# Every fourteenth group's first 128 rows fetched by SyncE, one row at a time

## The chip, the cores and the metric

The kernel runs on one core of a Trainium2 chip. A core has five engines, each with an instruction queue of its own: TensorE (PE in the profile, its weight loads PEld), VectorE (DVE), ScalarE (ACT), GpSimd (POOL) and SyncE (SP). SP computes nothing: here it issues transfers and waits for semaphores. Sixteen DMA engines carry out the transfers that the engines issue. Instructions of one engine go in order, and engines wait for each other by semaphores. The metric is the device time of one execution in microseconds (us), as a median of runs.

## The reference

A graph of 12,500 nodes with 128 features each and 200,000 edges, which are sorted by their destination node. Two layers follow a normalisation, and their result is added to the input:

```python
h = jnp.maximum(_layernorm(x, axis=-1), 0.0)
...
deg = jax.ops.segment_sum(jnp.ones_like(edge_weight_raw), dst, num_segments=N)
wsum = jax.ops.segment_sum(edge_weight_raw, dst, num_segments=N)
w = edge_weight_raw / jnp.maximum(wsum, EPS)[dst]
feat = jax.nn.relu(node_features @ W_pool + b_pool)
msg = feat[src] * w[:, None]
neigh = jax.ops.segment_max(msg, dst, num_segments=N)
neigh = jnp.where(deg[:, None] > 0, neigh, 0.0)
rst = node_features @ W1_self + neigh @ W1_neigh + b1
...
h = jax.nn.relu(rst)
msg2 = h[src] * w[:, None]
neigh2 = jax.ops.segment_sum(msg2, dst, num_segments=N) / jnp.maximum(deg, 1.0)[:, None]
out = jax.nn.relu(h @ W2_self + neigh2 @ W2_neigh + b2)
```

Layer 1 takes for each node the maximum of the weighted rows of its incoming edges' sources (`feat[src]`), layer 2 their weighted sum (`h[src]`). In both, 200,000 rows of 128 numbers (512 bytes) are read from a table in the chip's memory, in an order that only the input `src` tells.

## The kernel before

**Tiling.** The edges are cut into 391 groups of 512 (`NG`, the last with 320), and a group into four chunks of 128 (`Q`), one edge per partition. Nodes are worked on in 98 tiles of 128. The tables of the two layers are `feat_d` and `h_d`, each in the chip's memory.

**Gathers.** `gather` (L499 to L510) has GpSimd fetch the rows of a group into a buffer `gt`: one indirect DMA for each chunk (L507), whose 128 indices are a column of `srcT`. `sources` (L488 to L495) makes `srcT` in the preparation, from the loaded list of sources `sr`, in four parts: VectorE converts a part to floats (L491), TensorE transposes it, ScalarE writes it. SyncE isn't concerned with gathers.

**The ring.** `buffer` (L132) gives a group its place in a ring of buffers: 18 groups deep at first, then 14, then 11 (`full`), as tiles that were lent to it go back to other uses. Layer 2 has 11 throughout. GpSimd issues the gathers of group i as soon as the group that had that buffer has been read by TensorE, and so runs ahead of the other engines by as much as the ring is deep.

**Layer 1** is one loop over i (L860 to L980) whose order is written out by hand, since nothing reorders instructions there. Groups before 17 (`FIRST`) were gathered from x in the preparation; groups 17 to 390 are gathered from `feat_d` (L877). In iteration i TensorE transposes the four chunks of group i into PSUM (L896). VectorE multiplies by the edge weights `gs` (L940) and, one iteration later, takes the running maximum over each destination's edges with a scan (L911), with the marks `kt` that say where a destination begins. Two and more iterations later come transposes back (L952), a copy of ScalarE (L906), a product that picks each destination's last row (L961) and its copy into a window of the aggregate (L849). Finished node tiles pass through `nodes1` (L751 to L782), which stores `h_d` (L778).

**Layer 2** is a loop over i (L1050 to L1080). Group i is gathered from `h_d` (L1052), VectorE makes a small selection matrix with the weights in it (L996, L1001), TensorE multiplies each chunk by it one iteration later (`window_product`, L1008), and VectorE adds the result into the aggregate, at an address from a register (`window_add`, L1013; registers are loaded eight at a time, L729). Finished tiles pass through `nodes2` (L793 to L806), which stores the output four tiles at a time (L806); the input for the last addition is loaded four tiles at a time (L787).

**What SyncE does.** In layer 1 it issues in each iteration the load of `gs` for the next group (L583: 256 KB, three buffers, so it waits until L940 has used the group before the previous), every fourth iteration the load of `kt` (L589, 512 KB), and the stores of `h_d`. In layer 2 it issues L787 and L806 alone. A DMA that SyncE issues takes one of eight completion semaphores in turn; an engine that needs the data of several DMAs waits for each of their semaphores.

Of the kernel before, what the change touches and what calls it, by code (L numbers as in the profile page):

```python
# [7 lines left out]
F32 = mybir.dt.float32  # L8
# [30 lines left out]
LEAST = LESS + 4 * MID  # L39
KEPT = 4  # L40
PAIR = 2
PART = 24
PART_AT = (0, 1, 9, 17)
ADDED = PART_AT[-1] + PART
# [5 lines left out]
def gnn_kernel(ctx, tc, x, src, dst, ew, w_pool, b_pool, w1s, w1n, b1, w2s, w2n, b2, out):  # L50
# [29 lines left out]
    h_d = dram.tile([NP, D], F32, name="h_d")  # L80
    keep_d = dram.tile([NT * P, G], BF16, name="keep_d")
    s_d = dram.tile([2, NP], F32, name="s_d")

    one_way, other_way = (const.tile([P, NP + LW], F32, name=f"way_{i}") for i in range(2))
    h0T, h1T = (a[:, :NP].rearrange("p (t n) -> p t n", n=P) for a in (one_way, other_way))
# [402 lines left out]
    def sources():  # L488
        for t in range(NT):
            f = wk.tile([P, G], F32, name="sf")  # L490
            nc.vector.tensor_copy(f, sr[:, t, :])  # L491
            pt = columns(pq, f, Q)
            yield
            nc.scalar.activation(srcT[:, t], pt, AF.Copy)
            yield  # L495

    def edges_of(g):
# [4 lines left out]
    def gather(gt, table_d, g, only=None, last=None):  # L502

        t, r, ne, chunks = edges_of(g)
        limit = {} if last is None else dict(bounds_check=last, oob_is_err=False)
        for j, k in chunks if only is None else chunks[only:only + 1]:
            nc.gpsimd.indirect_dma_start(  # L507
                out=gt[:k, j, :], out_offset=None, in_=table_d[:, :],
                in_offset=bass.IndirectOffsetOnAxis(ap=srcT[:k, t, j, r:r + 1], axis=0), **limit)
        return gt  # L510
# [174 lines left out]
    def background():  # L685
# [8 lines left out]
            yield NG, fitness, t  # L694
        yield NG, lambda get, t: verdict(get), 0

    def pairs_of(g):
# [115 lines left out]
    with tc.manual_schedule(), tc.tile_pool(name="ew", bufs=3) as wk, \  # L813
# [3 lines left out]
        def side_step():  # L817

            while jobs:
                due, steps = jobs[0]  # L820
                if next(steps, jobs) is jobs:
                    jobs.pop(0)
                elif i < due:
                    break

        pms, scs, sels, prs, rws, pas = ({} for _ in range(6))
        turn = turns(wide1, 6)
        busy = {}

# [36 lines left out]
        for i in range(max(turn) + 6):  # L866
# [7 lines left out]
            if i % KEPT == 0 and i and i + 2 < NG:  # L874
                keep_rows(i + 2, keep_tile())
            if FIRST <= i < NG:
                gts[i] = gather(buffer(i, True), feat_d, i)  # L877

            if i + 1 < NG:
                weight_rows(i + 1, wk.tile([P, G], F32, name="gs"))  # L880
# [2 lines left out]
            if i < FIRST:  # L883
                if i > 0:
                    nc.scalar.activation(pms[i], raws.pop(i).rearrange("p q n -> p (q n)"), AF.Relu, bias=bp_col)
                if i + 1 < FIRST:
                    raw_columns(pn, i + 1)
                if i + 2 < FIRST:
                    raw_scale(i + 2)
                    raw_norm(i + 2)  # L890
                if i + 1 < FIRST:
                    raw_back(i + 1)
            elif i < NG:
                gt = gts.pop(i)
                for j, k in edges_of(i)[3]:
                    nc.tensor.transpose(pms[i][:, j * P:j * P + k], gt[:k, j, :], ident[:k, :k])  # L896
            if NG - 2 <= i < NG:
                window_copy(due(5))

# [73 lines left out]
                raw_stats(i + 3)  # L973
            if i >= FIRST and i % 3:
                side_step()
        assert not busy
        i = NG
        side_step()
# [4 lines left out]
    with tc.manual_schedule(), tc.tile_pool(name="ew2", bufs=3) as wk, \  # L983
            tc.tile_pool(name="ep2", bufs=2, space=PSUM) as ps:
        place = ps.tile([P, 2, Q, PART], F32, bufs=1)
        hit, iota = place[:, 0], place[:, 1]
        flip = ps.tile([P, 2, P], F32, bufs=1)
        for j, at in enumerate(PART_AT):
            nc.vector.tensor_copy(iota[:, j, :], cols[:, 0, at:at + PART])

        nc.vector.memset(agg2, 0.0)
        ss, pas, xrs = ({} for _ in range(3))

        def places(g):
            t, r, _, _ = edges_of(g)
            nc.vector.tensor_tensor(hit, iota, locT[:, t, :, r:r + 1].to_broadcast([P, Q, PART]), OP.is_equal)  # L996

        def weighted(g):
            t, r, _, _ = edges_of(g)
            ss[g] = wk.tile([P, Q, PART], F32, name="s")  # L1000
            nc.vector.tensor_tensor(ss[g], hit, w2T[:, t, :, r:r + 1].to_broadcast([P, Q, PART]), OP.mult)  # L1001

        def window_product(g):
            chunks = edges_of(g)[3]
            pas[g] = ps.tile([P, ADDED], F32, name="pa", bufs=3)
            gt, s = gts.pop(g), ss.pop(g)
            for j, k in reversed(chunks):
                nc.tensor.matmul(pas[g][:, PART_AT[j]:PART_AT[j] + PART], gt[:k, j, :], s[:k, j, :],  # L1008
                                 start=j == len(chunks) - 1, stop=j == 0, skip_group_check=True)

        def window_add(g, at):
            n = ADDED if g < GF else PART_AT[len(edges_of(g)[3]) - 1] + PART
            nc.vector.tensor_tensor(agg2[:, bass.ds(at, n)], pas.pop(g)[:, :n], agg2[:, bass.ds(at, n)], OP.add)  # L1013

        sbs = []
        for e in range(EARLY):
            sbs.append(wk.tile([P, G], I32, name=f"sb{e}", bufs=1))
            nc.sync.dma_start(sbs[e], src[None, e * G:(e + 1) * G].to_broadcast([P, G]))

        def early_groups():  # L1020

            for e in range(EARLY):
                one = dr.bitcast(F32)[:, :LATE, :G]
                for k in range(LATE):
                    nc.vector.tensor_scalar(one[:, k, :], sbs[e], late_nodes[:, k:k + 1], None, op0=OP.is_equal)
# [24 lines left out]
        for i in range(max(turn) + 2):  # L1050
            if EARLY <= i < NG:
                gts[i] = gather(buffer(i, False), h_d, i)  # L1052
                places(i)
            if EARLY <= i < NG:
                weighted(i)
            if i + 4 in turn:
                n = turn[i + 4]
                if n % wide2(n) == 0:
                    xr = x_rows(wk, n, wide2(n), 2)
                xrs[n] = xr  # L1060
            if late is not None:
                stages(late)
                late = None
            if i in turn:
                n = turn[i]
                late = nodes2(wk, ps, n, wide2(n), strided(agg2, n, wide2(n)), xrs.pop(n))
                next(late)
            g = i - 1
            if EARLY <= g < NG:
                window_product(g)  # L1070
            if i >= EARLY and i % 2:
                next(first_groups, None)
            if i == NG - 1:
# [128 lines left out]
```

## Time and profile before

| | us |
|---|---|
| median of 3 runs (4643.74 to 4653.1) | 4652.45 |
| the profiled execution | 4650.7 |
| its span, first to last instruction | 4648.7 |
| layer 1, gathers of L507 from `feat_d` into the ring | 190.3 to 2363.3 |
| layer 2, gathers of L507 from `h_d` into the ring | 2417.3 to 4623.6 |
| granted TensorE clock, mean of the span | 0.527 |

The profile is of one execution. A group row gives line, engine, operation, output and input, how often, busy time in all, mean nanoseconds of one, the idle time of the engine before these instructions and what ended most of it. In a timeline a row begins with the start and the duration in us, and ends with the idle time before it, in brackets. "Issue" is time in which an engine waited for nothing that the profile shows; "remote" is a releaser that the profile can't name. Rows of SPq and similar are instructions of an engine's queue, such as the issue of a DMA: not the transfer itself.

### The profile page before, as it was taken

The page shows a single profiled execution, that of the slowest core. Times are in us where ns is not written, and L with a number is a line of the kernel's source. Part 1 is how long each engine was busy: PE and PEld are TensorE (multiplying, and loading weights), DVE is VectorE, ACT ScalarE, POOL GpSimd, SP SyncE. Part 2 cuts the span into 40 slices and gives each one's busy share as a digit, 9 for nine tenths or more (in the row PEclk, how much of TensorE's full clock was granted, in tenths as well). Part 3 has the DMA queues.
Part 4 walks back from the last instruction along what each step waited for, and adds up shares of the span by engine and source line. Part 5 has one row for each costly group of instructions (what it writes and reads, how often), then busy time and mean ns, then how long its engine had stood idle before and what let it go on. Part 6 is the DMA issues. An engine that isn't in the chain of part 4 may idle for free.

```text
span 4648.7 us, 32678 instructions
## 1 busy us (share of the span) xinstructions
PE 1995.1 (43%) x8700; PEld 1817.3 (39%) x8700; DVE 1741.8 (37%) x5165; ACT 416.0 (9%) x1509; POOL 2953.3 (64%) x3143
## 2 busy tenths in 40 slices
PE   3654543444444444444453344334334333334334
PEld 2444433443434343433342334333334333333334
DVE  3676655765666566665560111111101111111111
ACT  3531111111111111111110000000000000000000
POOL 5356666666666666666646666666666666666665
PEclk8665555555555555555555555555555555555555
DMA  4333443444444444444431112112111111211111
GB/s 130 109 114 116 126 117 103 125 117 114 118 115 120 115 117 116 119 116 117 113 100 46 47 47 62 51 50 56 50 52 53 51 52 51 55 51 52 53 54 45
DMA packets 196303, 397.11 MB, mean 85 GB/s; under 512 B 60703, under 2 KB 69790, under 8 KB 196112
## 3 DMA queue, kind: packets, MB, share of 16 engines
q0 software_dynamic: 100032, 204.97, 17.3%
q1 hardware_dynamic: 95344, 189.06, 13.2%
q8 instruction: 73, 1.20, 0.1%
q10 hardware_dynamic: 736, 0.92, 0.1%
q14 instruction: 118, 0.97, 0.1%
HBM read 374.96 MB, written 19.77 MB: 85 GB/s over the span
## 4 chain that ended last, share of the span: by engine, by line
another core or an unknown queue 23%; issue 23%; PE 20%; POOL 19%; DVE 13%; DMA 1%; ACT 1%; POOLq 0%; ACTq 0%; DVEq 0%
POOL gt L507 18%; PE pa L1008 5%; PE pm L896 5%; DVE pm L911 4%; PE pn L961 4%; DVE pm L940 2%; PE pr L952 2%; DVE sc L936 1%; DVE sc L933 1%; DMA gt<-h_d,srcT 1%; DVE sel L922 1%; PE pn L743 1%; PE pf L643 1%; PE pn L780 1%
## 5 line engine op out<-in xcount | busy, mean ns | idle before, releaser
L507 POOL DMA_INDIRECT gt<-h_d,srcT x1551 | 1463.9, 944 | 743.6 <-issue 419.6
L507 POOL DMA_INDIRECT gt<-feat_d,srcT x1303 | 1230.0, 944 | 680.5 <-issue 294.5
L1008 PE MATMUL pa<-s,gt 128*128 128x24 f32 x3102 | 685.3, 382 | 734.4 <-remote 561.1
L1008 PEld LDWEIGHTS pa<-s,gt 128*128 128x128 f32 x3102 | 682.0, 330 | 748.7 <-remote 567.8
L1013 DVE TENSOR_TENSOR way<-pa,way 128x41 f32 x391 | 78.0, 199 | 1866.9 <-remote 1323.6
L896 PE MATMUL pm<-ident,gt 128*128 128x128 f32 (+1 forms) x1303 | 349.7, 423 | 521.5 <-issue 314.3
L940 DVE TENSOR_TENSOR pm<-pm,gs 128x512 f32<-128x512 f32 x390 | 271.1, 695 | 694.6 <-remote 529.1
L911 DVE TENSOR_TENSOR_SCAN pm<-kt,carry,pm 128x512 f32<-128x512 bf16 x389 | 496.3, 1276 | 4.0
L961 PEld LDWEIGHTS pn<-sel,rows 128*128 128x128 f32 x1564 | 368.8, 324 | 230.8 <-ACT way L849 128.2
L896 PEld LDWEIGHTS pm<-ident,gt 128*128 128x128 f32 (+1 forms) x1303 | 235.8, 218 | 560.4 <-issue 338.5
L961 PE MATMUL pn<-sel,rows 128*128 128x48 f32 x1564 | 358.2, 377 | 217.4 <-ACT way L849 121.9
L743 PE MATMUL pn<-w_2n,way 128*128 128x128 f32 x192 | 74.4, 491 | 601.3 <-issue 325.9
L743 PEld LDWEIGHTS pn<-w_2n,way 128*128 128x128 f32 x192 | 52.8, 323 | 620.2 <-issue 406.6
L906 ACT ACTIVATE rows<-pr 128x256 f32<-128x256 f32 x392 | 149.7, 383 | 1532.8 <-remote 662.1
L952 PE MATMUL pr<-ident,sc 128*128 128x128 f32 x782 | 241.8, 411 | 8.0 <-issue 3.9
L922 DVE TENSOR_SCALAR sel<-cols,lastT,invT 128x48 f32<-128x48 f32 x782 | 243.6, 312 | 0.0
L933 DVE COPY sc<-pm 128x256 f32<-128x256 f32 x391 | 162.6, 416 | 109.5 <-remote 85.9
L952 PEld LDWEIGHTS pr<-ident,sc 128*128 128x128 f32 x782 | 167.2, 224 | 11.5 <-issue 6.1
L936 DVE COPY_PREDICATED sc<-kt,pm 128x256 f32<-128x256 int16 x389 | 168.5, 433 | 4.9 <-issue 4.9
L507 POOL DMA_INDIRECT w2T<-feat_d,srcT x100 | 94.3, 943 | 105.8 <-DVE raw_mv L521 52.0
L780 PE MATMUL pn<-ident,h 128*128 128x128 f32 x94 | 41.9, 446 | 236.8 <-DVE ss L765 73.0
L780 PEld LDWEIGHTS pn<-ident,h 128*128 128x128 f32 x94 | 17.3, 184 | 270.1 <-issue 217.2
(273 smaller groups left out, 2079.6 us busy)
## 6 DMA issues: line engine op xcount, KB each, us to landing
gs<-in_edge_weight SPq DMA_DIRECT2D x389, 256.0 KB
kt<-keep_d SPq DMA_DIRECT2D x97, 512.0 KB
gt<-h_d,srcT POOLq DMA_INDIRECT x1551
gt<-feat_d,srcT POOLq DMA_INDIRECT x1303
feat_d<-fr SPq DMA_DIRECT2D x24, 256.0 KB
xr<-in_x SPq DMA_DIRECT2D x24, 256.0 KB
out<-o SPq DMA_DIRECT2D x24, 256.0 KB
h_d<-h SPq DMA_DIRECT2D x47, 128.0 KB
```

What stands on the lines that cost most here:

```text
L507: nc.gpsimd.indirect_dma_start(out=gt[:k, j, :], out_offset=None, in_=table_d[:, :], in_offset=bass.IndirectOffsetOnAxis(ap=srcT[:k, t, j, ...
L743: nc.tensor.matmul(po, nT, W[neigh_w], start=False, stop=True)
L896: nc.tensor.transpose(pms[i][:, j * P:j * P + k], gt[:k, j, :], ident[:k, :k])
L906: nc.scalar.activation(rws[g][:k, j, :], pr[:k, j, :], AF.Copy)
L911: nc.vector.tensor_tensor_scan(pm[:, :ne], kt[:, :ne], pm[:, :ne], carry, op0=OP.add, op1=OP.max)
L922: nc.vector.tensor_scalar(part, cols[:k, 1, :], lastT[:k, t, j, r:r + 1], invT[:k, t, j, r:r + 1], op0=OP.is_equal, op1=OP.mult)
L933: nc.vector.tensor_copy(sc[:, :ne // 2], two[:, :, 1])
L936: nc.vector.copy_predicated(sc[:, :ne // 2], new[:, :, 1], two[:, :, 0])
L940: nc.vector.tensor_tensor(pms[i][:, :n], rows[:, :n], ws.pop(i)[:, :n], OP.mult)
L952: nc.tensor.transpose(prs[g][:k, j, :], sc[:, j * P:j * P + k], ident)
L961: nc.tensor.matmul(pas[g], rows[:k, j, :], sel[:k, j, :], start=j == 0, stop=j == len(chunks) - 1)
L1008: nc.tensor.matmul(pas[g][:, PART_AT[j]:PART_AT[j] + PART], gt[:k, j, :], s[:k, j, :], start=j == len(chunks) - 1, stop=j == 0, skip_group ...
```

## The change

In preparation, `sources` also multiplies each source index by 512, its row's place in bytes in a table, and stores the four parts to a new table `at_d` in the chip's memory. A new class `Rows` takes chunk 0 of every fourteenth group away from the gathers: groups 37, 51, … 373 in layer 1 (25) and 20, 34, … 384 in layer 2 (27). For each such group g SyncE loads its 128 places, 512 bytes, into a small tile `listed`, at the end of iteration g - 18. In iterations g - 16 to g - 3 it then issues 128 DMAs of one row of 512 bytes each, nine or ten in an iteration, from the place that a register holds into one partition of a tile `single`; sixteen registers are loaded at a time (`BURST`). `single` and `listed` have two places each, used in turn. TensorE reads `single` instead of `gt` for chunk 0 of these groups, in both layers; their other three chunks, and all other groups, are gathered as before.

```diff
@@ sources
             nc.scalar.activation(srcT[:, t], pt, AF.Copy)
+            place = wk.tile([P, G], I32, name="sa")
+            nc.vector.tensor_scalar(place, sr[:, t, :], float(4 * D), None, op0=OP.mult)
+            nc.sync.dma_start(at_d[t * P:(t + 1) * P, :], place)
             yield
@@ gather
         for j, k in chunks if only is None else chunks[only:only + 1]:
+            if any(c.j == j and c.takes(g) for c in besides):
+                continue
             nc.gpsimd.indirect_dma_start(
@@ new
+    class Rows:
+
+        def __init__(self, wk, table, plane, every, first, end):
+            self.single = wk.tile([P, 2, D], F32, name="single", bufs=1)
+            self.listed = wk.tile([1, 2, P], I32, name="listed", bufs=1)
...
+            for c, g in enumerate(range(first, end, every)):
+                self.place[g] = c % 2
+                begin = g - every - 2
+                assert begin >= 2
+                self.plan.setdefault(begin - 2, []).append((self.load, g, 0))
+                for e in range(P):
+                    self.plan.setdefault(begin + e * every // P, []).append((self.fetch, g, e))
...
+        def rows(self, gt, g, j):
+            return self.single[:, self.place[g], :] if j == self.j and self.takes(g) else gt[:, j, :]
+
+        def load(self, g, _):
+            row = self.plane * NT * P + g
+            nc.sync.dma_start(self.listed[:, self.place[g], :], at_d[row:row + 1, self.j * P:(self.j + 1) * P])
+
+        def fetch(self, g, e):
+            if e % BURST == 0:
+                _, self.held = nc.values_load_multi_w_load_instructions(
+                    self.listed[:, self.place[g], e:e + BURST], [mybir.EngineType.SP], min_val=0,
...
+            at = self.held[e % BURST].with_bounds(min_val=0, max_val=(N - 1) * 4 * D, guaranteed_mod_val=0,
+                                                  out_of_modulus=4 * D)
+            nc.sync.dma_start(self.single[e:e + 1, self.place[g], :].bitcast(U8),
+                              self.flat[None, :].bitcast(U8)[:, bass.ds(at, 4 * D)])
+
+        def turn(self, i):
+            for step, g, e in self.plan.get(i, ()):
+                step(g, e)
@@ layer 1
+        byrow = Rows(wk, feat_d, 0, 14, FIRST + 14 + 6, NG - 4)
...
-                gts[i] = gather(buffer(i, True), feat_d, i)
+                gts[i] = gather(buffer(i, True), feat_d, i, besides=(byrow,))
...
-                    nc.tensor.transpose(pms[i][:, j * P:j * P + k], gt[:k, j, :], ident[:k, :k])
+                    nc.tensor.transpose(pms[i][:, j * P:j * P + k], byrow.rows(gt, i, j)[:k], ident[:k, :k])
...
+            byrow.turn(i)
@@ layer 2
+        byrow = Rows(wk, h_d, 0, 14, 14 + 6, NG - 4)
...
-                gts[i] = gather(buffer(i, False), h_d, i)
+                gts[i] = gather(buffer(i, False), h_d, i, besides=(byrow,))
...
-                nc.tensor.matmul(pas[g][:, PART_AT[j]:PART_AT[j] + PART], gt[:k, j, :], s[:k, j, :],
+                nc.tensor.matmul(pas[g][:, PART_AT[j]:PART_AT[j] + PART], byrow.rows(gt, g, j)[:k], s[:k, j, :],
...
+            byrow.turn(i)
```

More of the change, by code (lines that the diff above doesn't have):

```diff
@@ L41 @@
 PAIR = 2
+BURST = 16
 PART = 24
@@ L82, in gnn_kernel @@
     s_d = dram.tile([2, NP], F32, name="s_d")
+    at_d = dram.tile([NT * P, G], I32, name="at_d")
     one_way, other_way = (const.tile([P, NP + LW], F32, name=f"way_{i}") for i in range(2))
@@ L500, in edges_of, with gather @@
         return *divmod(g, P), ne, [(j, min(P, ne - j * P)) for j in range(-(-ne // P))]
-    def gather(gt, table_d, g, only=None, last=None):
+    def gather(gt, table_d, g, only=None, last=None, besides=()):
         t, r, ne, chunks = edges_of(g)
@@ L695, in background, with takes @@
         yield NG, lambda get, t: verdict(get), 0
+    class Rows:
+        def __init__(self, wk, table, plane, every, first, end):
+            self.single = wk.tile([P, 2, D], F32, name="single", bufs=1)
+            self.listed = wk.tile([1, 2, P], I32, name="listed", bufs=1)
+            self.plane, self.flat, self.j, self.place, self.plan, self.held = \
+                plane, table.rearrange("n d -> (n d)"), 0, {}, {}, {}
+            for c, g in enumerate(range(first, end, every)):
[5 more added lines that the diff above has]
+                    self.plan.setdefault(begin + e * every // P, []).append((self.fetch, g, e))
+        def takes(self, g):
+            return g in self.place
+        def rows(self, gt, g, j):
[7 more added lines that the diff above has]
+                    self.listed[:, self.place[g], e:e + BURST], [mybir.EngineType.SP], min_val=0,
+                    max_val=(N - 1) * 4 * D,
+                    skip_runtime_bounds_check_because="sources of edges are nodes, as the gathers have it")
+            at = self.held[e % BURST].with_bounds(min_val=0, max_val=(N - 1) * 4 * D, guaranteed_mod_val=0,
[5 more added lines that the diff above has]
+                step(g, e)
     def pairs_of(g):
```

## The prediction

> **What bounds the kernel now.** I read the busy table and the slices of the page first, then the costliest groups.
>
> ```profile
> PE 1995.1 (43%) x8700; PEld 1817.3 (39%) x8700; DVE 1741.8 (37%) x5165; ACT 416.0 (9%) x1509; POOL 2953.3 (64%) x3143
> ...
> DVE  3676655765666566665560111111101111111111
> ...
> POOL 5356666666666666666646666666666666666665
> ...
> another core or an unknown queue 23%; issue 23%; PE 20%; POOL 19%; DVE 13%; DMA 1%; ACT 1%; POOLq 0%; ACTq 0%; DVEq 0%
> ...
> L507 POOL DMA_INDIRECT gt<-h_d,srcT x1551 | 1463.9, 944 | 743.6 <-issue 419.6
> L507 POOL DMA_INDIRECT gt<-feat_d,srcT x1303 | 1230.0, 944 | 680.5 <-issue 294.5
> ```
>
> POOL is the busiest, at the same six tenths through both layers, and it does little but gather. The chain of waits names no bound: 23% of it ends at releasers that it can't name. So I looked at POOL's own rhythm, in the timeline of POOL in layer 2.
>
> ```profile
> 3436.67 0.94 POOL L507 DMA_INDIRECT gt<-h_d,srcT  x1 [0.30 <-issue]
> 3437.92 0.94 POOL L507 DMA_INDIRECT gt<-h_d,srcT  x1 [0.30 <-issue]
> 3439.17 0.94 POOL L507 DMA_INDIRECT gt<-h_d,srcT  x1 [0.30 <-issue]
> 3444.63 0.94 POOL L507 DMA_INDIRECT gt<-h_d,srcT  x1 [4.52 <-remote]
> ```
>
> A gather occupies POOL for 0.94 us, then 0.30 us pass: 1.25 us from start to start, 5.0 us for the four of a group. Now and then a longer stall comes (4.52 us here), at the first gather of a group: there POOL waits for a buffer of the ring. The windows give the pace with the stalls in it (first row: a special stretch, below; second: layer 1; third: layer 2; columns: PE, PE weight loads, DVE, ACT, POOL, clock, DMA share, GB/s).
>
> ```profile
> 802.00:824.70 22.70, 10.70 (x54) 9.31 (x54) 17.57 (x45) 5.17 (x19) 0.00 (x0) 0.58 0.31 90
> 850.00:2360.00 1510.00, 686.88 (x3012) 614.34 (x3010) 914.25 (x2276) 190.44 (x810) 987.30 (x1047) 0.51 0.42 117
> 2420.00:4624.00 2204.00, 848.55 (x3736) 817.91 (x3736) 272.93 (x1263) 0.00 (x0) 1461.32 (x1549) 0.50 0.19 52
> ```
>
> Layer 1: 1510 / 1047 = 1.442 us per gather, 5.77 us per group. Layer 2: 2204 / 1549 = 1.423, so 5.69. DVE is 61% busy in the one and 12% in the other, yet the pace is the same: what is common to both is POOL. The special stretch decides it. From 801.9 to 824.76 POOL stands still, because the ring shrinks there from 14 groups to 11. The consumers then run alone, on stored groups:
>
> ```profile
> 800.98 0.94 POOL L507 DMA_INDIRECT gt<-feat_d,srcT  x1 [0.30 <-issue]
> 824.76 0.94 POOL L507 DMA_INDIRECT gt<-feat_d,srcT  x1 [22.84 <-PE pm L896]
> ...
> 810.88 1.08 PE L896 MATMUL pm<-ident,w2T 128*128 128x128 f32 x4 [8.04 <-issue]
> 814.40 1.09 PE L896 MATMUL pm<-ident,w2T 128*128 128x128 f32 x4
> ...
> 820.98 1.08 PE L896 MATMUL pm<-ident,w2T 128*128 128x128 f32 x4 [1.84 <-issue]
> 824.04 1.09 PE L896 MATMUL pm<-ident,gt 128*128 128x128 f32 x4 [0.83 <-PE pn L961]
> ```
>
> PE begins a group every 3.1 to 3.5 us there, against 5.77 on the average. So POOL sets the pace and not PE, DVE or the weight loads of SP. The stalls on the ring's buffers do not contradict this: PE gives buffers back in bursts, around POOL's own pauses.
>
> ```profile
> 3429.77 1.87 PE L1008 MATMUL pa<-s,gt 128*128 128x24 f32 x8 [5.91 <-remote]
> 3444.40 0.20 DVE L1013 TENSOR_TENSOR way<-pa,way 128x41 f32 x1 [14.73 <-remote]
> 3445.17 1.02 PE L1008 MATMUL pa<-s,gt 128*128 128x24 f32 x4 [13.53 <-remote]
> ```
>
> After 3431.6 PE has no matmul until 3445.17, while POOL gathers on until 3440.1; then POOL stops, DVE and PE go on at 3444.4 and 3445.2, and POOL resumes at 3444.63. A stall is thus a tax on running far ahead, some 0.7 to 0.8 us a group (5.69 and 5.77 less 5.0).
>
> **The change part by part.** *Removed:* chunk 0 of 25 groups in layer 1 (37, 51, … 373) and 27 in layer 2 (20, 34, … 384), 52 of POOL's 3,143 instructions. Bounds of what one is worth: nothing, if the stall of the ring grows by what POOL saves; 1.25 us, if the stalls stay; 1.42 to 1.44 us, if the stalls shrink in proportion. For all 52: 0, 64.9, or 25 x 1.442 + 27 x 1.423 = 74.5 us. I take 64.9: the nearest row is the uninterrupted pitch, and the stall is as likely to stay as to shrink. What is late next is POOL still, with 55 gathers for 14 groups instead of 56.
>
> *Added on SP:* 128 fetches for each such group, 6,656 in all, over 14 iterations, thus 9.14 an iteration; a register load for every 16; 52 loads of a 512-byte list. These go at the end of iteration i, behind SP's own gs, kt, h_d, xr and out transfers of that iteration, and ahead of the next gs. No such fetch is in the trace. Nearest rows (timeline of SP, one-row transfers of the edge lists; groups of DMAs; register loads of eight values):
>
> ```profile
> 133.46 0.34 SPq L159 DMA_DIRECT2D dr<-in_dst  x1
> 133.84 0.25 SPq L165 DMA_DIRECT2D dr<-in_dst  x1
> 126.50 0.33 SPq L603 DMA_DIRECT2D feat_d<-fr  x1
> 126.87 0.44 SPq L159 DMA_DIRECT2D dr<-in_dst  x1
> ...
> L583 SPq DMA_DIRECT2D gs<-in_edge_weight x390: 327/328/793, 166.6 to 2391.2; - x195
> L589 SPq DMA_DIRECT2D kt<-keep_d x98: 320/327/435, 166.2 to 2387.5; - x98
> L729 DVEq TENSOR_LOAD <-bases x49: 593/596/1056, 2430.3 to 4625.9; - x49
> ```
>
> A one-row transfer is issued in 0.25 us, one of many rows in 0.33, or 0.44 when it follows another at once; 0.04 us lie between two (126.50 + 0.33 to 126.87). One load of eight registers is 0.60 us on DVE; for sixteen I estimate 0.6 to 1.2, so 0.04 to 0.08 a row. Low: 0.25 + 0.04 + 0.04 = 0.33 us a row. High: a row priced like the costliest gs issue, 0.79, and load: 0.87. I take 0.44, between the one-row record and a back-to-back transfer, with 0.04 gap and 0.06 load less the 0.10 by which one row is cheaper. SP's own work for 14 groups of layer 1 is 14 x (0.33 + 0.04) + 3.5 x 0.37 = 6.5 us, with under 1 us of others. With 128 x 0.44 = 56 it makes 63 of the 14 x 5.70 = 80 us that the new pace leaves; the point from which it no longer fits is (80 - 6.5) / 128 = 0.57 us a row. So I cost SP's rows at nothing: POOL's gathers cover them, and where that cover is gone, a row costs what it exceeds 0.57 by.
>
> [...]
>
> Queues that the rows are moved past: SP waits most of its time, and for DVE, one group after another, before each gs.
>
> ```profile
> SPq L583 <- DVE pm L940: 732.5, 121, 14.5
> SPq L806 <- DVE o L802: 548.4, 7, 97.3
> ```
>
> The rows of iteration i are queued behind those waits, so they go out only when DVE has got to group i - 2 of layer 1. The last ones for group g are of iteration g - 3, and PE needs them some four groups after that wait: 12 us or more, against 4 us of issue for nine rows. In layer 2 an out store holds SP for up to 97 us until DVE is there; it comes each 16 groups, and SP then issues 146 rows (64 us by the price taken) while the groups take 91. The gs load of the next group comes 4 us later than before; it has three buffers, 17 us, so nobody waits.
>
> *Added waits:* PE waits for a group's rows on up to eight semaphores, at the transposes and at the products of chunk 0. Behind them are that group's other work on PE, and through the ring POOL. A wait already satisfied is small change:
>
> ```profile
> L896 PEldq EVENT_SEMAPHORE  x374: 51/2946/13117, 283.8 to 2395.1; - x187
> L491 DVE CAST sf<-w2T x4: 417/418/426, 6.9 to 117.0; 128x512 f32<-128x512 int32 x4
> ```
>
> Seven more at 0.05 us are 0.36 us for 52 groups, 19 us at the outside, of which I take 2, since PE has 2 us a group to spare. The preparation gains four multiplies of the size of the cast above (0.42 us each) and four stores (0.33 us of issue): 0 to 5 us, taken as 3, because DVE is not full there (three and six tenths in its first two slices).
>
> Sum: the execution profiled took 4650.7 us (span 4648.7), 1.8 below the median of the runs, 4652.45. 4650.7 - 64.9 + 2 + 3 = **4591 us**.
>
> **Rivals.** *A, the time comes back as ring waits.* POOL reaches the full ring sooner and waits for PE's next burst. For it: the stalls sit at the first gather of a group and end with PE, remote waits of 470 us in all:
>
> ```profile
> POOL gt L507 <- remote: 470.1, 224, 7.5
> ```
>
> Against it: the consumers alone need 3.1 us. If a saved gather gave 40% back, it would be 52 x 0.75 = 39 us, 4617; if all, 4650.7 + 5 = 4656, no change.
>
> *B, SP becomes the bound, slower.* From 0.57 us a row the rows set the pace of PE, and POOL waits for the ring. At 0.62 a group takes (6.5 + 128 x 0.62) / 14 = 6.13 us, 0.40 over the mean of 5.73, for some 377 + 387 groups less the 40 outside the schedule: +290, thus 4940; at 0.60, 5.95 and +160, 4810; at the high end of 0.87 about 6,600. For it: a price with a register as offset isn't shown, and it needs only 0.13 more than I take. Against it: 0.25 for a one-row transfer.
>
> *C, completions in the way.* While POOL gathers, PE's progress stands for 13 us (above). If 9 small completions an iteration hold it in the same manner, each stall grows. Stalls are 0.7 us a group; with 14 completions where there were five, I price it at a third of that more, 0.24 us for 720 groups: +170 less 65, 4755. Against it: the special stretch, in which DMA moved 90 GB/s without POOL, went smoothly, and layer 1, with far more SP transfers, stalls hardly more than layer 2.
>
> That the rows aren't taken off POOL at all I exclude: the gather skips the chunk where it is issued.
>
> **How the numbers follow.** Forecast 0.57 (4572 to 4612: from 4650.7 less the 74.5 of shrinking stalls and 4 of noise, to the start of A); A 0.20, of which 0.09 still faster; B 0.14; C 0.09. About 0.2%, 9.3 us, is what a measurement of this kernel can tell from no change. Faster 0.57 + 0.09 = 0.66; same 0.11 of A and 0.01 of C = 0.12; slower 0.14 + 0.08 = 0.22. The range of 8 in 10 holds C and leaves out most of B, and 0.03 below: 4570 to 4760.
>
> **What would show it.** POOL's gathers go from 1,303 and 1,551 to 1,278 and 1,524, their pitch stays at 1.25 us, and the two windows keep 1.42 to 1.45 us a gather (forecast); A shows as longer remote stalls, B as SP without idle time, with row issues of 0.55 us and up, and PE waiting at L896 and L1008 for SP's DMAs in each fourteenth group; C as longer stalls in all groups with SP idle. I am wrong if a row's issue takes over 0.57 us from start to start, or if the pitch of POOL's gathers itself grows while SP issues.

## The result, and the profile after

| | before, us | change, us | ratio (95% interval) |
|---|---|---|---|
| first comparison | 4652.77 | 5521.61 (5493.17 to 5537.84) | 1.186 (1.181 to 1.192) |

The change is slower by 869 us, 18.6%. The forecast was 4591, with a range of 4570 to 4760, and the time lies far above it. The direction is that of rival B. The profiled execution has a span of 5536.0 us.

The page of the changed kernel, its busy table and its groups of gathers (L514 is the old L507; last column: idle time of POOL before these instructions and what ended most of it):

```profile
PE 1987.4 (36%) x8700; PEld 1827.7 (33%) x8700; DVE 1758.4 (32%) x5169; ACT 425.3 (8%) x1509; POOL 2903.6 (52%) x3091
...
L514 POOL DMA_INDIRECT gt<-h_d,srcT x1524 | 1437.9, 943 | 1218.8 <-PE pa L1057 559.5
L514 POOL DMA_INDIRECT gt<-feat_d,srcT x1284 | 1211.6, 944 | 1077.4 <-PE pm L944 644.8
```

The 52 gathers are gone (3,091 instructions for 3,143), and one still takes 0.944 us. (The row of layer 1 has 1,284 and not the 1,278 named in the prediction, since 6 of the 25 were gathers into tiles that were lent to the ring, which have rows of their own.) But POOL stands idle 1219 us among layer 2's gathers, where it was 744. Who waits for whom in the changed kernel (columns: us in all, times, longest):

```profile
DVE pm L988 <- DMA gs<-in_edge_weight: 1019.3, 241, 12.6
...
PE pa L1057 <- DMA single<-h_d: 882.3, 27, 51.8
```

In layer 2 PE waits at each of the 27 groups, up to 52 us, until the last of its 128 rows is there. In layer 1 it hardly waits for rows (27.0 us in all, five times). There VectorE waits for the edge weights `gs`, because SP issues `gs` behind the rows and is late with everything. SP's own waits, which were 732 us for L940 before, are nearly gone:

```profile
SPq L590 <- DVE pm L988: 65.0, 53, 8.9
```

So SP is the bound. The instructions of L737, the line that issues the rows, show their price (columns of durations: least, median, longest, in ns; then the first and the last start in us):

```profile
L737 SPq MOVE single<-h_d x3456: 1/29/1424, 2845.1 to 5509.9; - x192
L737 SPq DMA_DIRECT2D single<-h_d x3456: 1/228/1441, 2846.5 to 5510.0; - x192
```

A row is a register move and a DMA. From the first to the last, (5510.0 - 2846.5) / 3456 = 0.77 us a row, against the 0.44 forecast and the 0.57 from which it no longer fits. Yet the median is only 0.029 + 0.228. The mean is made by instructions of up to 1.4 us, and these are register moves as well as DMAs. The timeline of SP, and that of POOL in the same stretch (a row x9 stands for nine in sequence):

```profile
1501.17 6.89 SPq L737 DMA_DIRECT2D single<-feat_d  x9
...
1510.32 3.59 SPq L737 DMA_DIRECT2D single<-feat_d  x10
```

```profile
1503.95 0.94 POOL L514 DMA_INDIRECT gt<-feat_d,srcT  x1 [0.30 <-issue]
1508.33 0.94 POOL L514 DMA_INDIRECT gt<-feat_d,srcT  x1 [3.43 <-PE pm L944]
```

POOL gathers until 1504.9 and pauses until 1508.33. Nine rows issued at the end of that run and just behind it take 6.89 us; ten rows issued from 1510.32 on take 3.59, though POOL gathers again by then: what holds SP begins and ends later than the gathers. That gave the theories for the experiments: SP is held by POOL's gathers (theory 1), or a row with a register as its offset simply costs 0.77 (the rival).

### The profile page after: what moved, and what is told of

The parts are those of the page before. It is cut to its first block, busy times and chain, and to the rows that moved or that the text cites. A ratio compares the mean times of both kernels' runs of the same rounds, so it can differ in the third digit from the quotient of the medians.

```text
span 5536.0 us, 46822 instructions
## 1 busy us (share of the span) xinstructions
PE 1987.4 (36%) x8700; PEld 1827.7 (33%) x8700; DVE 1758.4 (32%) x5169; ACT 425.3 (8%) x1509; POOL 2903.6 (52%) x3091
## 5 line engine op out<-in xcount | busy, mean ns | idle before, releaser
L514 POOL DMA_INDIRECT gt<-h_d,srcT x1524 | 1437.9, 943 | 1218.8 <-PE pa L1057 559.5
L514 POOL DMA_INDIRECT gt<-feat_d,srcT x1284 | 1211.6, 944 | 1077.4 <-PE pm L944 644.8
L1057 PE MATMUL pa<-s,gt 128*128 128x24 f32 x3048 | 669.4, 382 | 511.6 <-remote 414.5
L1057 PEld LDWEIGHTS pa<-s,gt 128*128 128x128 f32 x3048 | 669.2, 331 | 518.2 <-remote 420.4
L988 DVE TENSOR_TENSOR pm<-pm,gs 128x512 f32<-128x512 f32 x390 | 272.3, 698 | 1203.9 <-DMA gs<-in_edge_weight 1019.3
L944 PE MATMUL pm<-ident,gt 128*128 128x128 f32 x1284 | 345.9, 423 | 770.7 <-issue 688.6
L944 PEld LDWEIGHTS pm<-ident,gt 128*128 128x128 f32 x1284 | 230.7, 216 | 811.1 <-issue 720.8
L1057 PE MATMUL pa<-s,single 128*128 128x24 f32 x54 | 16.1, 386 | 882.3 <-DMA single<-h_d 882.3
L1057 PEld LDWEIGHTS pa<-s,single 128*128 128x128 f32 x54 | 13.5, 311 | 884.9 <-issue 579.3
L794 PE MATMUL pn<-w_2s,way 128*128 128x128 f32 x192 | 76.7, 503 | 254.6 <-DVE o L849 230.8
```

Of the source, the lines that this page charges most:

```text
L514: nc.gpsimd.indirect_dma_start(out=gt[:k, j, :], out_offset=None, in_=table_d[:, :], in_offset=bass.IndirectOffsetOnAxis(ap=srcT[:k, t, j, ...
L944: nc.tensor.transpose(pms[i][:, j * P:j * P + k], byrow.rows(gt, i, j)[:k], ident[:k, :k])
L988: nc.vector.tensor_tensor(pms[i][:, :n], rows[:, :n], ws.pop(i)[:, :n], OP.mult)
L1057: nc.tensor.matmul(pas[g][:, PART_AT[j]:PART_AT[j] + PART], byrow.rows(gt, g, j)[:k], s[:k, j, :], start=j == len(chunks) - 1, stop=j == 0 ...
```

## The experiments

The experiments ran on several chips. On one of them the kernel before takes 3944 us, on the others 4614 to 4653, so each is compared with runs of the kernel before on its own chip. The first four fell on the one with 3944, which was met that one time. Whether the difference belongs to the chip or to a state that it was in then, the runs don't show. The others are called chips with holds below, since instructions turn out to be held there.

**e1: no rows.** The fetches are left out, the gathers are those of the change.

```diff
+            nc.vector.memset(self.single, 0.0)
...
         def turn(self, i):
-            for step, g, e in self.plan.get(i, ()):
-                step(g, e)
+            pass
```

> Chunk 0 of the 52 groups is neither gathered nor fetched: its tile stays zero, so that part of the computation is left out. POOL issues the same 52 gathers fewer as in the changed kernel, and SP issues no row. Theory 1 (POOL sets the pace, and all that the change lost is due to SP's rows): 4650 less 52 x 1.25 = 65 and plus 2 for the preparation, about 4588 (4578 to 4600). Rival (the time of a gather left out comes back as a wait for the ring): 4640 to 4655. If it stays above 5000, the loss has nothing to do with the rows.

3882.44 against 3944.40, ratio 0.984 (0.983 to 0.986): 62 us saved. The expectation had 65 for 52 gathers, on another base time.

**e2: half the rows.**

```diff
+            nc.vector.memset(self.single, 0.0)
...
-                for e in range(P):
-                    self.plan.setdefault(begin + e * every // P, []).append((self.fetch, g, e))
+                for e in range(P // 2):
+                    self.plan.setdefault(begin + 2 * e * every // P, []).append((self.fetch, g, e))
```

> Of the 128 rows of each of the 52 groups only 64 are fetched, spread over the same 14 iterations (the other 64 stay zero: that part of the computation is left out); the gathers are those of the changed kernel. The trace of the changed kernel has 0.77 us from row to row, so 4.6 rows an iteration are 3.5 us, and with 0.5 us of other work SP is done in 4.0 of the 5.7 us of a group. Theory 1 (the loss is SP's rate alone): SP has time to spare again and the time is near that without rows, 4585 to 4620. Rival (each row holds the other engines, whatever SP's rate): half of the loss of 870 us stays, about 5030.

3880.26, ratio 0.984 (0.982 to 0.985): 64 us saved, as without rows. On this chip 3,328 rows cost nothing that can be measured.

**e3: layer 2 without gathers.**

```diff
-                gts[i] = gather(buffer(i, False), h_d, i, besides=(byrow,))
+                gts[i] = buffer(i, False)
```

> The gathers of layer 2's loop are left out, so that TensorE multiplies what layer 1 left in the buffers; SP's rows stay, all of them, and layer 1 is unchanged. In the trace of the changed kernel a row is 0.32 us after the row before in stretches where POOL has stood for some us, and often 0.7 or 1.4 us later where POOL has gathered for over 5 us. Theory 1 (POOL's gathers hold SP's transfers): in layer 2 a row falls to 0.36 to 0.42 us with the register loads, 14 groups to 50 or 55 us, and layer 2 from 2664 us to 1350 to 1600; the whole to 4200 to 4450. Rival (0.77 us is what a row costs SP by itself, by its register, its semaphore or the one DMA queue): layer 2 keeps 2600 us or more, the whole 5400 or more.

3481.62, timed once; the totals of e1 to e4 had been worked out from 4650 and are to be read from 3944. Its layer 1, where gathers and rows are both as in the change, answers more than its layer 2: there are no long moves or DMAs even beside gathers.

```profile
L737 SPq MOVE single<-feat_d x3200: 29/29/38, 201.2 to 1912.2; - x189
L737 SPq DMA_DIRECT2D single<-feat_d x3200: 227/228/378, 201.3 to 1912.2; - x189
```

And POOL there gathers without a stall. This is the window 700 to 1900 of e3 (PE, PE weight loads, DVE, ACT, POOL, clock, DMA share, GB/s): 1200 / 961 = 1.249 us a gather, the bare pitch.

```profile
700.00:1900.00 1200.00, 640.53 (x2814) 582.08 (x2814) 866.54 (x2137) 186.06 (x760) 906.71 (x961) 0.50 0.50 138
```

So on this chip SP keeps up with all rows of layer 1.

**e4: every 28th group.**

```diff
-        byrow = Rows(wk, feat_d, 0, 14, FIRST + 14 + 6, NG - 4)
+        byrow = Rows(wk, feat_d, 0, 28, FIRST + 28 + 6, NG - 4)
...
-        byrow = Rows(wk, h_d, 0, 14, 14 + 6, NG - 4)
+        byrow = Rows(wk, h_d, 0, 28, 28 + 6, NG - 4)
```

> Every 28th group instead of every 14th: 26 groups give up chunk 0, and SP issues 128 rows in 28 iterations, 4.6 an iteration. Nothing of the computation is left out. At 0.77 us a row SP needs 3.5 us and 0.5 us of other work in the 5.7 us of a group. Theory 1 (rate alone): SP fits, and the saving is 26 x 1.25 = 32 us: about 4622 (4605 to 4640), faster than before. Rival (each row holds the others): slower than before, 5030 or so. Rival (time given back at the ring): 4640 to 4655.

3912.68, ratio 0.992 (0.991 to 0.994): 32 us saved for 26 gathers, 1.22 each.

**r1, r2, g3, i3, j1, k1: the change again, and the kernel before with its profile.** None of these runs fell on the chip of 3944, so their first cases stay untested.

> The changed kernel as it is. On the chip of the first four experiments the kernel before takes 3944 us and not 4652, and a row costs SP 0.32 us with no stall of 0.7 us anywhere. Theory 1 (the loss came from a condition of the first chip in which instructions are held for 0.7 us while POOL gathers; without it SP fits): where the kernel before takes about 3944, the change takes 3944 less 62 to 65, 3875 to 3890; where it takes about 4650, the change takes about 5520 again. Rival (full rows are too many for SP anywhere): at least 4000 where the kernel before takes 3944.

> The kernel before as it is, for its profile beside r1. Theory 1: where it takes about 3944, POOL's gathers follow each other at 1.25 us without a stall at the ring (3074 x 1.25 = 3840 and little else), and the engines that wait for them have no waits beyond the gathers' landing; where it takes about 4650, the stalls of the ring come each four to eleven groups as in the first profile. Rival: the same stalls at the ring, only shorter.

> The changed kernel as it is. Where the kernel before takes 3944: 3875 to 3890, as r1 was to show. Where it takes 4640: 5500 again.

> The changed kernel as it is. Where the kernel before takes 3944: 3875 to 3890. Where it takes 4640: 5500 again.

> The changed kernel as it is, once more, for a chip on which the kernel before takes 3944: 3875 to 3890 there (theory: without holds SP's rows cost 0.40 us with their register loads, 51 us of 14 groups' 69). Where the kernel before takes 4610 to 4650: 5400 to 5520 as on four such chips.

> The changed kernel as it is, on the chip of k2. Where the kernel before takes 3944: 3875 to 3890. Where it takes 4610 to 4650: 5400 to 5520.

| | before, us | change, us | ratio (95% interval) |
|---|---|---|---|
| r1 | 4641.58 | 5504.85 | 1.184 (1.181 to 1.188) |
| g3 | 4647.21 | 5508.02 | 1.187 (1.183 to 1.191) |
| i3 | 4614.54 | 5419.91 | 1.174 (1.169 to 1.179) |
| j1 | 4618.57 | 5433.42 | 1.178 (1.174 to 1.182) |
| k1 (chip of j1) | 4642.51 | 5499.59 | 1.182 (1.177 to 1.187) |

The loss is 17 to 19% on all of them. r2 took 4641.69, and POOL's idle time among layer 2's gathers is 740 us, as in the first profile (744). On the chip of 3944 POOL has no stalls there: e1's row of gathers there, and that of i1 (below), the same kernel on one of the others.

```profile
L514 POOL DMA_INDIRECT gt<-h_d,srcT x1524 | 1437.9, 944 | 464.4 <-issue 422.7
```

```profile
L514 POOL DMA_INDIRECT gt<-h_d,srcT x1524 | 1440.2, 945 | 717.9 <-issue 415.1
```

464.4 / 1524 is 0.305 us, the gap after each gather and nothing else; 717.9 has 253 us of stalls on top.

**g1: layer 2 without gathers, on a chip of 4647.** The edit is that of e3.

> As e3: layer 2's gathers left out, TensorE multiplies what layer 1 left in the buffers, all SP rows kept. On a chip where the kernel before takes 4640: theory 1 (POOL's gathers hold SP) has layer 1 as slow as in the change, to about 2750 us, and in layer 2 rows at 0.40 us without stalls, 14 groups in some 54 us, so 1450 us as in e3: 4250 in all. Rival (SP is slow on that chip by itself): layer 2 takes 2600 or more, 5400 in all. Where the kernel before takes 3944: 3480 again.

4308.85, timed once (expected 4250). One execution shows both prices, layer 1 with gathers and layer 2 without:

```profile
L737 SPq MOVE single<-h_d x3456: 29/29/29, 2821.4 to 4280.2; - x192
L737 SPq DMA_DIRECT2D single<-h_d x3456: 227/228/288, 2821.5 to 4280.3; - x192
L737 SPq MOVE single<-feat_d x3200: 1/29/1410, 295.3 to 2723.2; - x189
L737 SPq DMA_DIRECT2D single<-feat_d x3200: 1/228/1411, 295.3 to 2723.9; - x189
```

Without gathers 1458.8 / 3456 = 0.42 us a row with the register loads, and every move takes 29 ns. With gathers 2428.6 / 3200 = 0.76. So on such a chip SP is held while POOL gathers and not otherwise: theory 1 stands, and the rival, a row's own price, falls.

**h1: copies on an idle engine.** What is held, the way to the DMA engines, or any instruction?

```diff
+        tick = wk.tile([P, 1], F32, name="tick", bufs=1)
...
             if EARLY <= i < NG:
                 weighted(i)
+            if EARLY <= i < NG:
+                for _ in range(12):
+                    nc.scalar.activation(tick, cols[:, 0, 0:1], AF.Copy)
```

> The kernel before, with twelve copies of one column into a tile that nobody reads added on ScalarE in each of the 388 iterations of layer 2's loop. ScalarE is idle there, nothing waits for the copies, they move no data by DMA and signal nobody; all they add is instructions, 24 starts and ends in the records of a group beside some 60. Layer 1 is untouched. Theory R (on the slow chips it is the recording of instructions and semaphores that falls behind while POOL gathers, and holds the engines): where the kernel before takes 4640, layer 2 grows by a tenth or more, 200 us and up, and the copies show durations or gaps in steps of 0.7 us; where it takes 3944, no change. Theory F (what falls behind is the way by which POOL and SP reach the DMA engines and semaphores, and instructions as such cost nothing): no change on either, within 10 us, and copies of one even duration.

4666.20 against 4647.21, ratio 1.005 (1.003 to 1.007): between the two theories, far nearer to no change. But the copies themselves come in steps (ScalarE's timeline; the number in brackets is the idle time before):

```profile
3406.08 0.20 ACT L1059 ACTIVATE tick<-cols 128x1 f32<-128x1 f32 x1 [0.51 <-ACT tick L1059]
3406.80 0.20 ACT L1059 ACTIVATE tick<-cols 128x1 f32<-128x1 f32 x1 [0.51 <-ACT tick L1059]
...
3412.43 7.76 ACT L1059 ACTIVATE tick<-cols 128x1 f32<-128x1 f32 x33 [0.49 <-ACT tick L1059]
```

0.20 + 0.51 is the same 0.7 us, and then 33 copies go at 0.24 us each. By theory R this was to cost 200 us, the author's estimate; 19 is against it, if the limit is one that all engines share. The expectation said that the copies signal nobody. That was mistaken: they all wrote one tile, and so each raised a semaphore for the next (ScalarE waited for `tick` 838.6 us in all, 1,153 times).

**h2: copies that wait for nothing and signal nothing.**

```diff
+        ticks = wk.tile([P, 10 * (NG - EARLY)], BF16, name="ticks", bufs=1)
...
+                for k in range(10):
+                    k += 10 * (i - EARLY)
+                    nc.scalar.activation(ticks[:, k:k + 1], cols[:, 0, 0:1], AF.Copy)
```

> As h1, but ten copies an iteration, each into a column of its own, so that none waits for another and none raises a semaphore; nothing orders them, so ScalarE runs all 3880 of them from the start of layer 2 on, one after the other. In h1 on a slow chip the copies, each of which waited for the one before by a semaphore, came 0.24 us apart while POOL paused and 0.7 us apart after 5 us of gathers. Theory S (what is late is the updates of semaphores): these copies come at one even distance of 0.25 us or less on any chip, and the time is within 10 us of before. Theory R (instructions themselves are held, by their records): on a chip where the kernel before takes 4640 they too come 0.7 us apart in POOL's long runs; on one where it takes 3944 at an even distance.

4626.15 against 4614.54, ratio 1.003 (1.002 to 1.004). ScalarE's timeline inside a run of gathers, in a pause of POOL, and after the start of the next pause; then POOL's:

```profile
2440.37 0.20 ACT L1060 ACTIVATE ticks<-cols 128x1 bf16<-128x1 f32 x1 [1.20 <-issue]
2441.77 0.20 ACT L1060 ACTIVATE ticks<-cols 128x1 bf16<-128x1 f32 x1 [1.20 <-issue]
2443.17 0.20 ACT L1060 ACTIVATE ticks<-cols 128x1 bf16<-128x1 f32 x1 [1.20 <-issue]
...
2463.47 0.20 ACT L1060 ACTIVATE ticks<-cols 128x1 bf16<-128x1 f32 x1 [1.20 <-issue]
2464.87 0.20 ACT L1060 ACTIVATE ticks<-cols 128x1 bf16<-128x1 f32 x1 [1.20 <-issue]
...
2474.67 3.71 ACT L1060 ACTIVATE ticks<-cols 128x1 bf16<-128x1 f32 x36 [0.49 <-issue]
```

```profile
2466.55 0.94 POOL L507 DMA_INDIRECT gt<-h_d,srcT  x1 [7.17 <-remote]
...
2470.30 0.94 POOL L507 DMA_INDIRECT gt<-h_d,srcT  x1 [0.30 <-issue]
2475.17 0.94 POOL L507 DMA_INDIRECT gt<-h_d,srcT  x1 [3.93 <-PE pa L1009]
```

The copies use no DMA and no semaphore and wait for nobody. In the lines shown they come 1.40 us apart, twice 0.70; elsewhere 0.70 (from 2420.07 us) and 2.10 (from 2423.57) occur as well. The hold doesn't end with the gathers: it goes on through POOL's pause of 7.17 us before 2466.55. In the next pause it ends 3.4 us after POOL's last gather, and then 36 copies take 3.71 us, most of them while POOL gathers again. Theory S falls: instructions as such are held, on an engine that has nothing to do with POOL. That they are loaded too late is unlikely: the page of h2 lists 221 packets of instructions (73 and 148) for 36,563 instructions, too few for a step at each copy.

Theory R, that it is the recording of instructions, stays a conjecture of the author's. No run here was without records (the granted clock that stands with each timed run is read from them), so what the kernels take unrecorded isn't shown. After h1 it could only be a limit of each engine by itself. To count a start and an end for each copy, at 0.70 us each, agrees with the 1.40 us shown here, but not with the 0.7 us shown for h1's copies, so the count doesn't settle it either.

**i1, i2: e1 and e2 on a chip with holds.**

> As e1: chunk 0 of the 52 groups is neither gathered nor fetched, so that part is left out. Where the kernel before takes 4640: if the gathers alone set the pace there, as the forecast had it, 4640 less 52 x 1.25 to 1.44, so 4568 to 4580. Rival (the time of a gather left out comes back as a longer hold): 4630 to 4650. Where it takes 3944: 3882 again.

> As e2: half the rows of the 52 groups are fetched, the other half stay zero. Where the kernel before takes 4640: every 28th group with all its rows gave 4652 against 4647 there, no gain, at the same 4.6 rows an iteration. If rows cost the others 26 x 1.35 = 35 us at that rate whatever was taken off POOL, this one gains what i1 gains less 35 to 40, 4605 to 4620. Rival (rows at 4.6 an iteration already leave SP no time): no gain here either, 4640 to 4660. Where it takes 3944: 3880 again.

i1 4545.39 against 4614.54, ratio 0.986 (0.984 to 0.988): 69 us saved by 52 gathers left out. i2 4583.08, ratio 0.993 (0.991 to 0.994): 31 saved. Both expectations are to be read from 4614.54 in place of 4640, and both hold. The 3,328 rows cost 38 us, 0.011 us a row. The expectation had SP with time to spare, but the waits of i2 say that it was often late: VectorE waited for `gs` behind the rows, a wait that i1 doesn't have, and SP's own wait for VectorE before it issues `gs` is 58 us, where i1 has 439 (L590, L988 and L989 are L583 and L940 of the kernel before).

```profile
DVE pm L989 <- DMA gs<-in_edge_weight: 228.9, 76, 11.0
SPq L590 <- DVE pm L989: 58.1, 20, 7.5
```

**g2, j2: every 28th and every 20th group on chips with holds.** The edits are those of e4, with 20 for 28 in j2.

> As e4: every 28th group, 26 groups, nothing left out. Where the kernel before takes 4640: theory 1 (rate alone; 4.6 rows an iteration at 0.77 us are 3.5 us, with other work 4.0 of 5.7) gives a saving of 26 x 1.25 to 1.43, so 4600 to 4615. Rival (while rows are issued they are held at 0.9 us and more, and hold the others in turn): slower than before, from 4700 up. Where it takes 3944: 3912 again.

> Every 20th group: 37 groups give up chunk 0, 6.4 rows an iteration, nothing left out. Where the kernel before takes 3944: 3944 less 37 x 1.25, 3898 (3893 to 3905). Where it takes 4610 to 4650: at 0.77 us a row and 0.5 of other work SP would still fit, 5.4 of 5.7 us, and the kernel would be near before (within 20 us, as at 4.6 rows); if it is slower by over 100 us, the price of a row rises as SP falls behind.

g2 4651.68, ratio 1.001 (0.999 to 1.003): neither of its two cases. 26 gathers are worth 26 x 69 / 52 = 35 us, and 3,328 rows take 37 by i2's price: nothing is left, and that is what was measured (on another chip than i2). j2 4793.16, ratio 1.039 (1.037 to 1.041): 175 us lost at 6.4 rows an iteration, where 0.77 a row would have fitted. The price is not a constant. The window of layer 1 in j2 (POOL's gathers; us, POOL busy and count, clock, DMA share, GB/s):

```profile
850.00:2360.00 1510.00, 939.16 (x996) 0.51 0.41 113
```

With 79 gathers for 20 groups that is 1510 / 996 x 79 / 20 = 5.99 us a group. SP's own work by the prediction is 6.5 x 20 / 14 = 9.3 us, so a row takes (20 x 5.99 - 9.3) / 128 = 0.86 us. POOL gathers 996 x 1.25 / 1510 = 82% of the time there. In the change a row takes 0.72 us in layer 1 (worked out below), with POOL gathering 948 x 1.25 / 1700 = 70%. In these two cases a row costs more where POOL gathers more, and with fewer rows it does.

**k2: rows of layer 2 from two engines.**

```diff
-            nc.sync.dma_start(self.single[e:e + 1, self.place[g], :].bitcast(U8),
+            (nc.scalar if e % self.queues else nc.sync).dma_start(
+                self.single[e:e + 1, self.place[g], :].bitcast(U8),
...
-        byrow = Rows(wk, h_d, 0, 14, 14 + 6, NG - 4)
+        byrow = Rows(wk, h_d, 0, 14, 14 + 6, NG - 4, 2)
```

> In layer 2 alone, where ScalarE is idle, it issues every second row of the 27 groups (and loads the same registers); SyncE issues the others. Layer 1 is the change's. Nothing is left out. Where the kernel before takes 4610 to 4650: if each engine is held by itself, one start or end of an instruction per 0.7 us, 4.6 rows an iteration fit on each, as they did with half the rows (i2), and layer 2 goes from 2610 us back to 2200 to 2280: 5000 to 5100 in all. Rival (the engines share one limit): layer 2 stays, 5400. Where before takes 3944: 3875 to 3890.

5046.41 against 5499.59 for the change on the same chip; against before 1.087 (1.085 to 1.089). It came out as expected if each engine is held by itself; a limit that both share at 0.77 us a row would have left layer 2 as it was. ScalarE's rows, and PE's wait for rows (882.3 us in the first profile of the change):

```profile
L739 ACTq DMA_DIRECT2D single<-h_d x1728: 3/228/1479, 2807.8 to 5008.1; - x192
...
PE pa L1060 <- DMA single<-h_d: 17.6, 4, 7.6
```

They come 2200.3 / 1728 = 1.27 us apart, SP's as well, 0.64 for the two together, and layer 2 is back at some 2,200 us. The 1.27 is no price of a row but the pace of the loop, in which PE hardly waits for rows any more. Layer 1, where SP issues all rows, keeps its loss (its last row starts at 2712.5 us, in the first profile of the change at 2736.0).

## Why the prediction was wrong

**What bounds the kernel: half right.** That a gather left out saves about its pitch held: 69 us on a chip with holds (i1), 62 on the one without, against 64.9 forecast from bounds of 0 and 74.5. Rival A, time given back at the ring, fell. But the stalls were read as "a tax on running far ahead". On the chip of 3944 the ring is as deep and POOL has no stall. The reading that fits the runs, though none tested it, is that the stalls come of the holds: the engines behind POOL are late while it gathers, and give buffers back when it pauses.

**The price of a row: the step that failed.** I took 0.44 us, "between the one-row record and a back-to-back transfer". SP undisturbed takes 0.42 (g1), so the sum of the rows was good for an SP that nothing holds. The sixteen registers cost more than I put in (0.06 a row, 0.96 in all): a register load takes 1.22 us in the changed kernel, just above the 0.6 to 1.2.

```profile
L731 SPq TENSOR_LOAD <-listed x416: 3/1220/1593, 297.8 to 5503.7; - x139
```

Beside POOL's gathers the same row took 0.77 us in layer 2 of the change and 0.76 in layer 1 of g1, past the 0.57 from which it no longer fits. What was missing is the state of the machine in which the rows would be issued. The one-row transfer that I priced by is from the preparation, at 134 us, and POOL stood still there from 115.07 to 167.04:

```profile
167.04 0.94 POOL L507 DMA_INDIRECT w2T<-feat_d,srcT  x1 [51.97 <-DVE raw_mv L521]
```

In the loops POOL gathers seven eighths of the time (1549 x 1.25 of 2204 us in layer 2 before), and there many an instruction of SP takes 0.7 us longer, or twice that: in the change a row's move has a median of 0.029 us and a longest of 1.42, and undisturbed it takes 0.029 each time (g1). SP's few transfers in the loop before hardly showed it: the `gs` issues have a median of 0.33 us and a longest of 0.79. But the prediction had a sign of it and quoted it: PE without a matmul for 13 us while "POOL gathers on". It put that down to running far ahead, and in C to something that more completions might lengthen, and didn't ask whether SP, with 18 new instructions an iteration, would stand still like PE.

**"So I cost SP's rows at nothing".** The cover went with the price. By the pace of the change (windows of its gathers; us, POOL busy and count, clock, DMA share, GB/s):

```profile
900.00:2600.00 1700.00, 894.11 (x948) 0.50 0.34 97
2900.00:5200.00 2300.00, 1247.98 (x1323) 0.50 0.16 43
```

1700 / 948 x 55 / 14 = 7.05 us a group in layer 1 and 6.83 in layer 2, so 0.72 us a row in layer 1 by the prediction's own formula, (14 x 7.05 - 6.5) / 128. Rival B had this: SP as the bound, the point from which it decides (0.57) and the form of the sum; it had a chance of 0.14. With 0.72 its sum gives (6.5 + 128 x 0.72) / 14 = 7.05 us a group and, for its 724 groups, some 5,600 in all, where 5,522 was measured. Its reason for the price, the register as offset, is not the one found (0.42 in g1). Its place in layer 1 was off: not PE at L896 but VectorE at L940 waits, for `gs` queued behind the rows. "So nobody waits" for that `gs` was wrong as well.

**The number of transfers** is not the cause by itself: undisturbed, layer 1's 3,200 rows fit beside the gathers (e3, with 1.249 us a gather), and layer 2's take 128 x 0.42 = 54 us of 80 (g1).

**Rival C**, longer stalls in all groups with SP idle, isn't shown. Where nothing is held it fell: 3,328 rows cost nothing (e2), and POOL keeps its bare pitch, 1.249 us, beside all rows of layer 1 (e3). On a chip with holds 3,328 rows cost 38 us (i2), but SP was late with `gs` there, which is cause enough; whether a part of it is C's was not taken apart.

**The added waits and the preparation**, 5 us, can't be told apart from the rest: e1 has the preparation, but not the waits, and saves 62 of 65.

Not measured: the change itself where nothing is held. e3's layer 1 and e1, e2 and e4 speak for some 3,880 there, an estimate.

## What to carry to other kernels

A price is taken from rows in the state in which the new work will run: an engine that was idle, or one seen in the preparation alone, need not tell what it costs beside the loop's load. Look at what the other engines did when the row was taken. If any engine stands still while another is busy, ask whether an instruction added elsewhere would stand still too. And a moved load is judged by the slack of the engine that takes it at its held price, and by everything that this engine also issues for others, such as `gs` here.

## What the runs showed of the hardware

The same kernel took 3944 us on one chip, met once, and 4614 to 4653 on the others. A gather into the ring takes 0.944 us in e1 on the one and 0.943 to 0.945 on the others (change, h1, i1), and the granted clock doesn't tell them apart (0.518 in e1, 0.523 in i1). On the others, instructions of SyncE and ScalarE, a register move and a copy that waits for nobody among them, were held in steps of about 0.70 us while POOL gathered: a move of 0.029 us took up to 1.42 (change), and h2's copies came 0.70, 1.40 or 2.10 us apart. In k2 SyncE and ScalarE each issued a row in 1.27 us, 0.64 for the two together, which speaks against a limit of 0.77 us a row that both share. The hold outlasts the gathers: in h2 it went on through a pause of 7.17 us, ended 3.4 us into the next, and then 36 copies took 3.71 us, most of them while POOL gathered again. What makes it isn't shown. Every 28th group saves 32 us on the one chip (e4) and nothing on the other on which it ran (g2, ratio 1.001), and none of the versions that leave nothing out beats the kernel before where there are holds.
